# Attention in strict program order with layer 2 in slots beside the heads, and Mamba's side work in other slots

## The chip, the cores and the metric

The kernel runs on one core of a Trainium2 chip. The metric is device time in microseconds of one execution. Times before come from three runs and one profiled execution; a profile is one execution with every instruction recorded. Engines are named as in the profile: PE (matmuls), PEld (PE's weight loads), DVE (vector), ACT (scalar, with the exponentials), POOL (GpSimd), SP (issues DMAs).

## The reference, cut to what matters

For a batch of 8 images of 256 channels and 1024 positions, in float32:

```python
for i in range(4):                                   # four Mamba layers
    xs = xs + mamba(layernorm(xs), ...)              # state scan over 1024 positions, 512 channels x 16 states
y  = xo * sigmoid(se(xo.mean((2, 3)))) + residual    # squeeze and excite
x  = batchnorm(y)                                    # over all 8 images

# layer 1: 4 heads of 64
attn = softmax(einsum('bihd,bjhd->bijh', q, k) * 64 ** -0.5, over j)
x = (attn @ v) @ w_out + b_out + x
# layer 2: one head of 256, and the maximum minus the energy
energy = q @ k.T
attention = softmax(energy.max(-1) - energy)
x = gamma * (attention @ v) + x
# layer 3: 8 heads of 32
tok = x + position_encoding
out = softmax(q @ k.T / 32 ** 0.5) @ v @ Wo + bo
```

## The kernel before

**Two phases.** `mamba_phase` runs the four Mamba layers, the gate and the statistics of the batch norm and leaves y in DRAM (`spill`). `attention_phase` then reads each image back, normalises it and runs the three attention layers. A general attention after it runs only if a range check fails, which it does not with these inputs. At the phases' border the SBUF pools change, so attention's loads start when Mamba's last work is done.

**Order in Mamba.** Its `nc` is `Engines(tc)`: every instruction of PE, DVE, ACT and POOL is kept in program order; SP's DMAs are not. A unit is one half image (512 positions) of one layer: 64 units, each of 16 steps. A step forms two inputs `bx` on PE from a diagonal matrix `dg` and the transposed `dtxT`, scans each on DVE (`h`), multiplies by C on POOL, and sums over states on PE (`y`, three steps later). Beside the steps run the pieces of other units: `inward` (layer norm, input projections `pin`, convolution taps, gate `sz`, projection `pp`) for the unit two ahead, `onward` (`pb`, `pd`, softplus, `dtx`) and `turn` (transposes `pt`) for the next, `outward` (`po`, residual, and in the last layer the gate) for the one before. A unit has 64 slots, four per step, and `BESIDE_SCAN` says at which slot each piece of a stage stands; `DIAGONALS` does so for the loads of `dg`. Slots a and b of a step (0 and 1 modulo 4) stand before its first `bx` and after its second, c and d follow. The small PSUM pool `ps_m` has two buffers, for `pmu`, `pvar`, `pin`, `pp`, `pb`, `pd`, `pt` and `po`.

**Order in attention.** Its `nc` is the plain `tc.nc`: the framework's scheduler puts each engine's instructions in an order of its own choice, within dependencies and the buffers of the pools. The outer order is layer 1 of image 0, layer 1 of image 1, layer 3 of image 0, layer 1 of image 2, layer 3 of image 1, and so on. `heads` (line 643) is the work of one layer 1 or 3: 32 steps, each with scores `fs` for one key tile of 128 and half the queries (line 655; two heads of 64 rows, or four of 32 rows), one or two exponentials to `fp` (660), the product with v to `fo` (671) and the sums of the weights to `fz` (677, on DVE, and for the second pair of heads on POOL). Every eighth step the sums are added over partitions by a matmul with ones (`fzs`, 688), inverted (690) and multiplied in (692), and POOL checks their range (695, 696). `LAG` is the number of steps by which product and sum follow the scores.

Beside the heads of one layer runs `beside(i)` (line 787): the end of the layer before (`residual`, then all of `layer2`; or `output`) and the beginning of the layer after (`begin`: load, batch norm, q, k, v; or q, k, v of layer 3), as one sequence of pieces, dealt out evenly by the counts in `BESIDE`. `layer2` goes over eight query tiles: energies (735) into a score buffer, minimum (738), exponential with sum (741), a diagonal matrix `dg` with gamma over the sum (747), the transpose and scaling in one as a matmul with `dg` (753), two copies (754), the product with v (759), the residual (761).

Score buffers `ps_s`: two, of 128x1024, for `fs` of layers 1 and 3 and for layer 2's energies. All other PSUM tiles of attention: four buffers of `ps_o`. The pool `pp` has six buffers for `fp`, each with the weights of one pair of heads in one step.

Of the kernel before, what the change touches and what calls it, by code (L numbers as in the profile page):

```python
# [12 lines left out]
F32 = mybir.dt.float32  # L13
AF = mybir.ActivationFunctionType
# [5 lines left out]
P = 128  # L20
# [32 lines left out]
class Engines:  # L53
# [12 lines left out]
BESIDE_SCAN = (  # L66
    ("weights", 2, (2, 2, 3, 4)),
    ("onward", 1, (3, 5, 8, 12, 12, 13, 21, 25, 27, 31, 35, 35, 41, 46, 46, 51)),
    ("turn", 1, (49, 51, 55, 57)),
    ("outward", -1, (6, 12, 16, 18, 21, 29, 31, 32, 39, 43, 50, 51, 55, 55, 61)),  # L70
    ("inward", 2, (2, 4, 7, 10, 16, 21, 23, 25, 28, 34, 40, 40, 44, 44, 44, 46, 49, 59, 63)),
)

DIAGONALS = (16, 20, 36, 40, 44, 48, 52, 56)

# [481 lines left out]

LAG = {1: 3, 2: 2}

BESIDE = {(0, 1): 13, (1, 3): 49, (1, 1): 50, (3, 3): 16, (3, 0): 4}  # L560


def attention_phase(tc, ctx, a, spill, ident, gvec, stats, out, top):

    nc = tc.nc
    cst = ctx.enter_context(tc.tile_pool(name="f_cst", bufs=1))
    xp = ctx.enter_context(tc.tile_pool(name="f_x", bufs=4))
    qp = ctx.enter_context(tc.tile_pool(name="f_q", bufs=3))
    kp = ctx.enter_context(tc.tile_pool(name="f_k", bufs=2))
    pp = ctx.enter_context(tc.tile_pool(name="f_p", bufs=6))  # L570
    zp = ctx.enter_context(tc.tile_pool(name="f_z", bufs=3))
# [9 lines left out]

    w = {k: load(k, [P, CT, C], a[k]) for k in ATT_W if k not in ("wq2", "wk2")}
    pe = load("pe", [P, CT, HW], a["pe"])
    bv = {n: load(f"bv{n}", [P, C], a[f"bv{n}"].partition_broadcast(P)) for n in (1, 2, 3)}
    gamma = load("gamma", [P, 1], a["gamma"].partition_broadcast(P))
    ones = cst.tile([P, 64], F32, name="ones")
    nc.gpsimd.memset(ones, 1.0)
    ok = cst.tile([P, T], F32, name="ok")
    nc.gpsimd.memset(ok, 1.0)
    mv, bsc = bn_scale(nc, cst, gvec, stats)  # L590

    def gcol(i):
        return gvec[:, i:i + 1]

    rows = [load(k, [P, CT, C], a[k]) for k in ("wq2_rows", "wk2_rows")]
    w["wq2"] = cst.tile([P, CT, C], F32, name="wqk2")
    bias2 = cst.tile([P, CT], F32, name="bias2")
    for m in range(CT):  # L600
        ps = ps_o.tile([P, T], F32, name=f"wqk2_{m}", tag="o")
        for k in range(CT):
            nc.tensor.matmul(ps[:, :C], lhsT=rows[0][:, k, m * P:(m + 1) * P], rhs=rows[1][:, k, :],
                             start=(k == 0), stop=(k == CT - 1))
        nc.vector.tensor_copy(w["wq2"][:, m, :], ps[:, :C])
        ps = ps_o.tile([P, T], F32, name=f"bias2_{m}", tag="o")
        for k in range(CT):
            nc.tensor.matmul(ps[:, :1], lhsT=rows[1][:, k, m * P:(m + 1) * P], rhs=gcol(G_BQ2 + k),
                             start=(k == 0), stop=(k == CT - 1))
        nc.vector.tensor_copy(bias2[:, m:m + 1], ps[:, :1])  # L610

# [30 lines left out]
    def heads(n, b, s, D, scale):  # L642
# [20 lines left out]
        def product(i):  # L663
            m, half, kt = steps[i]
            if kt == 0:
                acc["o"] = ps_o.tile([P, T], F32, name=f"fo{u}_{m}_{half}", tag="o")
                acc["z"] = [zp.tile([P, 2, T], F32, name=f"fz{u}_{m}_{half}_{j}", tag="z") for j in range(pairs)]
            ps = probs[i]
            for h in range(2 * pairs):
                r = h * D  # L670
                nc.tensor.matmul(acc["o"][r:r + D, :], lhsT=v[:, kt, m * P + r:m * P + r + D], rhs=ps[h // 2][:, h % 2, :],  # L671
                                 start=(kt == 0), stop=(kt == TT - 1))

            if kt:
                for j in range(pairs):
                    add = nc.gpsimd.tensor_tensor if j else nc.vector.tensor_tensor
                    add(acc["z"][j], acc["z"][j] if kt > 1 else probs[i - 1][j], ps[j], ALU.add)  # L677
                del probs[i - 1]

        def divide(i):  # L680
            m, half, kt = steps[i]
            if kt < TT - 1:
                return
            del probs[i]
            z = ps_o.tile([P, T], F32, name=f"fzs{u}_{m}_{half}", tag="o")
            for h in range(2 * pairs):
                r = h * D
                nc.tensor.matmul(z[r:r + D, :], lhsT=ones[:, :D], rhs=acc["z"][h // 2][:, h % 2, :], start=True, stop=True)  # L688
            rec = sp.tile([P, T], F32, name=f"frec{u}_{m}_{half}", tag="rec")
            nc.vector.reciprocal(rec, z)  # L690

            nc.vector.tensor_tensor(q[:, m, half * T:(half + 1) * T], acc["o"], rec, ALU.mult)
            for op, bound in ((ALU.is_le, 1e25), (ALU.is_ge, 1e-37)):
                f = sp.tile([P, T], F32, name=f"fok{u}_{m}_{half}_{bound}", tag="f")
                nc.gpsimd.tensor_scalar(f, rec, bound, None, op)
                nc.gpsimd.tensor_tensor(ok, ok, f, ALU.mult)

        lag = LAG[pairs]
        for i in range(len(steps) + lag + 1):
            if i < len(steps):  # L700
                weights(i)
            if 0 <= i - lag - 1:
                divide(i - lag - 1)
            if lag <= i < len(steps) + lag:
                product(i - lag)
            yield

# [18 lines left out]
    def layer2(b, x):  # L726
        s = {}
        yield from qkv(2, b, x, bias2, None, s)
        q, v = s["q"], s["v"]
        for t in range(TT):  # L730
            u = f"{b}_{t}"
            sc = ps_s.tile([P, 2, T], F32, name=f"fs2{u}", tag="s")
            for half in range(2):
                for m in range(CT):
                    nc.tensor.matmul(sc[:, half, :], lhsT=q[:, m, t * P:(t + 1) * P], rhs=x[:, m, half * T:(half + 1) * T],  # L735
                                     start=(m == 0), stop=(m == CT - 1))
            e = l2.tile([P, 1], F32, name=f"fe2{u}", tag="e")
            nc.vector.tensor_reduce(e, sc, AX.XY, ALU.min)
            p = l2.tile([P, HW], F32, name=f"fp2{u}", tag="p2")
            z = l2.tile([P, 1], F32, name=f"fz2{u}", tag="z")  # L740
            nc.scalar.activation(p, sc.rearrange("p h t -> p (h t)"), AF.Exp, bias=e, scale=-1.0, accum_out=z)  # L741
            yield

            rz = l2.tile([P, 1], F32, name=f"frz2{u}", tag="rz")
            nc.vector.reciprocal(rz, z)
            dg = l2.tile([P, P], F32, name=f"fdg2{u}", tag="dg")
            nc.vector.tensor_scalar(dg, ident, rz, gamma, ALU.mult, ALU.mult)
            pt = l2.tile([P, TT, P], F32, name=f"fpt2{u}", tag="pt")
            for g in range(2):
                ps = ps_o.tile([P, TT // 2, P], F32, name=f"ft2{u}_{g}", tag="o")  # L750
                for j in range(TT // 2):
                    kt = g * TT // 2 + j
                    nc.tensor.matmul(ps[:, j, :], lhsT=p[:, kt * P:(kt + 1) * P], rhs=dg, start=True, stop=True)  # L753
                nc.vector.tensor_copy(pt[:, g * TT // 2:(g + 1) * TT // 2, :], ps)
            yield
            po = ps_o.tile([P, CT, P], F32, name=f"fo2{u}", tag="o")
            for m in range(CT):
                for kt in range(TT):
                    nc.tensor.matmul(po[:, m, :], lhsT=v[:, kt, m * P:(m + 1) * P], rhs=pt[:, kt, :],  # L759
                                     start=(kt == 0), stop=(kt == TT - 1))  # L760
            nc.vector.tensor_tensor(s["q"][:, :, t * P:(t + 1) * P], po, x[:, :, t * P:(t + 1) * P], ALU.add)
            yield
# [3 lines left out]

    xs = {}

    def begin(b, s):
        x = xs[b] = xp.tile([P, CT, HW], F32, name=f"fx{b}", tag="x")  # L770
        for h in range(NCH):
            nc.sync.dma_start(x[:, :, h * T:(h + 1) * T], spill[b][h])
        for m in range(CT):
            nc.vector.tensor_scalar(x[:, m, :], x[:, m, :], mv[:, m, 0:1], bsc[:, m:m + 1], ALU.subtract, ALU.mult)
            nc.vector.tensor_scalar(x[:, m, :], x[:, m, :], gcol(G_BNB + m), None, ALU.add)
        yield
        yield from qkv(1, b, x, gvec[:, G_BQ1:G_BQ1 + CT], gvec[:, G_BK1:G_BK1 + CT], s)
# [8 lines left out]

    def beside(i):
        if i:
# [4 lines left out]
            else:  # L793
                yield from output(b, state[3, b])
        if i + 1 < len(order):
            n, b = order[i + 1]
# [5 lines left out]
    for _ in begin(0, state[1, 0]):  # L802
        pass
    for i, (n, b) in enumerate(order):
        side = beside(i)
        D = 64 if n == 1 else 32
        count = CT * 2 * TT
        work = BESIDE[(order[i - 1][0] if i else 0, order[i + 1][0] if i + 1 < len(order) else 0)]
        done = 0
        for g, _ in enumerate(heads(n, b, state[n, b], D, D ** -0.5)):  # L810
            while done * count < work * (g + 1):
                next(side, None)
                done += 1
        for _ in side:
            pass
# [304 lines left out]
```

## Time and profile before

| what | value |
|---|---|
| runs | 9191.63, 9197.91, 9198.4 us, median 9197.91 |
| profiled execution | 9194.97 us |
| its span, first to last instruction | 9193.1 us |
| last PE work of Mamba ends (`se`) | about 6543 us |
| first attention matmul (`wqk`) starts | 6574.01 us |
| first projection of layer 1 (`fwq`) starts | 6580.22 us |
| layer 3's heads of image 1 (with layer 2 of image 2 beside them) | 7223.4 to 7447.2 us |
| layer 1's heads of image 3 | 7447.2 to 7546.9 us |
| mean granted clock of PE | 0.975 |

The page's lines for groups name the line of the kernel, engine, operation, output and inputs, shapes, and the idle time before. In Mamba all lines are L48, the helper that records each operation, so groups are told apart by their tiles. A float32 matmul shows as two PE instructions.

What some groups of attention cost (from 7000 to 9000 us; busy us, mean ns, then idle before and what ended it):

```profile
L660 ACT ACTIVATE fp<-fs 128x1024 f32<-128x1024 f32 x592 | 590.2, 1022 | 1096.8 <-PE fs L655 1085.5 <-POOL ok L696 11.3
L677 POOL TENSOR_TENSOR fz<-fz,fp 128x1024 f32<-128x1024 f32 x149 | 366.6, 2461 | 373.8 <-ACT fp L660 371.9
L690 DVE RECIPROCAL frec<-fzs 128x512 f32<-128x512 f32 x49 | 164.5, 3356 | 58.0 <-PE fzs L688 57.1
L753 PE MATMUL ft<-fdg,fp 128*128 128x128 f32 x816 | 115.1, 297 | 3.8 <-DVE frec L690 3.8
L747 DVE TENSOR_SCALAR fdg<-ident,frz,gamma 128x128 f32<-128x128 f32 x52 | 18.0, 346 | 1.9
```

### The profile page before, as it was taken

Reading aid. Unit: us, or ns where it says so; the run is one execution under the profiler, and the core shown is the slowest. Engines: PE = TensorE matmul, PEld = TensorE weight load, DVE = VectorE, ACT = ScalarE, POOL = GpSimd, SP = SyncE. Lnnn points to the kernel's source line nnn. Section 1 sums busy time; section 2 is a strip of 40 time slices with the busy share of each in tenths; the row PEclk is TensorE's granted clock in tenths of the full one; section 3 lists DMA queues with packets and bytes.
Section 4 is the critical chain, followed back from the end, with each engine's and each line's share of the span. In section 5 each row is a group of like instructions: output and inputs, shape, how many; then the busy total and the mean of one; then the engine's idle time right before and its main releaser. Section 6 shows DMA issues by size and latency. Waiting matters only on the chain.

```text
span 9193.1 us, 231133 instructions
## 1 busy us (share of the span) xinstructions
PE 8829.2 (96%) x100850; PEld 4513.2 (49%) x100850; DVE 7154.2 (78%) x7267; ACT 5369.8 (58%) x7646; POOL 7009.5 (76%) x2696
## 2 busy tenths in 40 slices
PE   8999999999999999999999999999799999999998
PEld 4555555555555555555555555555344334434433
DVE  5898988889888898989889999999654554455455
ACT  6667676766776676676667677767323333333334
POOL 5999999999999999999999999999414343343436
PEclk8999999999999999999999999999999999999999
DMA  3434434443443444344444444444200000000000
GB/s 108 129 120 122 124 122 127 121 127 122 122 122 124 127 121 127 122 122 123 123 127 121 137 134 134 135 130 141 99 1 5 10 10 5 5 5 5 1 5 10
DMA packets 559192, 845.58 MB, mean 92 GB/s; under 512 B 311456, under 2 KB 312544, under 8 KB 557536
## 3 DMA queue, kind: packets, MB, share of 16 engines
q1 hardware_dynamic: 558176, 830.71, 29.6%
q8 instruction: 799, 13.09, 0.6%
q14 instruction: 217, 1.78, 0.1%
HBM read 771.31 MB, written 59.24 MB: 90 GB/s over the span
## 4 chain that ended last, share of the span: by engine, by line
PE 86%; DVE 6%; ACT 3%; POOL 2%; issue 2%; DMA 0%; SPq 0%; ACTq 0%; DVEq 0%; POOLq 0%
PE bx L48 20%; PE y L48 19%; PE pin L48 10%; PE fs L655 6%; PE po L48 5%; PE fo L671 4%; DVE h L48 3%; PE fo L759 3%; PE pp L48 3%; PE fs L735 3%; PE pd L48 2%; PE fwq L615 2%; PE fwv L637 2%; PE ft L753 1%; PE pvar L48 1%
## 5 line engine op out<-in xcount | busy, mean ns | idle before, releaser
L48 POOL TENSOR_TENSOR h<-h,ct 128x2048 f32<-128x2048 f32 x1024 | 4640.3, 4544 | 451.9 <-PE y L48 161.3
L48 ACT ACTIVATE da<-dt,A 128x512 f32<-128x512 f32 x4096 | 2642.6, 713 | 224.9 <-DVE h L48 222.6
L48 DVE TENSOR_TENSOR_SCAN h<-da,hc,bx 128x512 f32<-128x512 f32 x2048 | 2456.8, 1261 | 238.8 <-PE bx L48 228.4
L48 DVE TENSOR_TENSOR_SCAN h<-da,bx 128x512 f32<-128x512 f32 x2048 | 2356.9, 1203 | 281.1 <-PE bx L48 266.3
L48 PEld LDWEIGHTS bx<-dg,dtxT 64*64 64x64 f32 x65536 | 1915.0, 135 | 1264.1 <-issue 1178.1
L48 PE MATMUL bx<-dg,dtxT 64*64 64x128 f32 x65536 | 2253.4, 276 | 39.7 <-DVE h L48 28.8
L48 PE MATMUL y<-h,twin 64*64 64x512 f32 x16384 | 2018.8, 608 | 6.1 <-POOL h L48 6.1
L660 ACT ACTIVATE fp<-fs 128x1024 f32<-128x1024 f32 x768 | 765.6, 1022 | 1426.3 <-PE fs L655 1398.0
L48 PE MATMUL pin<-xn,win 128*128 128x512 f32 x2048 | 1009.2, 616 | 61.4 <-ACT sz L48 49.4
L48 PEld LDWEIGHTS y<-h,twin 64*64 64x64 f32 x16384 | 616.1, 138 | 675.6 <-issue 665.8
L677 POOL TENSOR_TENSOR fz<-fz,fp 128x1024 f32<-128x1024 f32 x192 | 478.1, 2490 | 414.5 <-ACT fp L660 410.5
L677 DVE TENSOR_TENSOR fz<-fz,fp 128x1024 f32<-128x1024 f32 x384 | 531.8, 1385 | 328.0 <-ACT fp L660 323.7
L655 PE MATMUL fs<-fq,fk 32*128 32x512 f32 (+1 forms) x3072 | 718.0, 646 | 54.9 <-ACT fp L741 39.3
L48 DVE SCALAR_TENSOR_TENSOR xin<-pin,vec,xin 128x509 f32<-128x509 f32 (+2 forms) x768 | 571.6, 744 | 100.3 <-ACT xin L48 42.8
L671 PE MATMUL fo<-fp,fv 128*32 128x512 f32 (+1 forms) x3072 | 596.6, 615 | 0.0
L48 PEld LDWEIGHTS pin<-xn,win 128*128 128x128 f32 x2048 | 355.6, 191 | 457.9 <-issue 330.4
L48 ACT ACTIVATE xin<-pin,cb,vec 128x512 f32<-128x512 f32 x256 | 199.2, 778 | 621.8 <-PE pin L48 621.8
L48 PE MATMUL po<-sz,wo 128*128 128x512 f32 x1024 | 500.7, 612 | 0.0
L48 ACT ACTIVATE sz<-pin,ib 128x512 f32<-128x512 f32 x256 | 175.9, 687 | 549.8 <-PE pin L48 549.8
L655 PEld LDWEIGHTS fs<-fq,fk 32*128 32x128 f32 (+1 forms) x3072 | 195.3, 185 | 467.8 <-issue 271.0
L677 POOL TENSOR_TENSOR fz<-fp,fp 128x1024 f32<-128x1024 f32 x32 | 83.1, 2597 | 403.2 <-PE fzs L688 240.8
L48 ACT ACTIVATE e<-pd,vec 128x512 f32<-128x512 f32 x256 | 176.1, 688 | 317.4 <-PE pd L48 312.5
(391 smaller groups left out, 8743.4 us busy)
## 6 DMA issues: line engine op xcount, KB each, us to landing
ct<-cdr SPq DMA_DIRECT2D x1024, 512.0 KB, 3.9
dg<-diagonals SPq DMA_DIRECT2D x512, 256.0 KB, 4.3
spill<-xo SPq DMA_DIRECT2D x72, 512.0 KB, 5.3
x<-spill SPq DMA_DIRECT2D x48, 512.0 KB, 7.8
xo<-spill SPq DMA_DIRECT2D x48, 512.0 KB, 5.0
x<-in_x SPq DMA_DIRECT2D x16, 512.0 KB, 8.4
res<-in_x SPq DMA_DIRECT2D x16, 512.0 KB, 5.1
diagonals<-bt SPq DMA_DIRECT2D x512, 4.0 KB, 4.6
```

The costliest lines, as they stand in the source:

```text
L48: return self.tc.keep_in_program_order(getattr(self.engine, name)(*args, **kwargs))
L615: nc.tensor.matmul(ps, lhsT=wt[:, k, m * P:(m + 1) * P], rhs=x[:, k, half * T:(half + 1) * T], start=(k == 0), stop=(k == CT - 1))
L637: nc.tensor.matmul(ps[:, j, :], lhsT=x[:, kc, (t + j) * P:(t + j + 1) * P], rhs=w[f"wv{n}"][:, kc, :], start=(kc == 0), stop=(kc == CT - 1))
L655: nc.tensor.matmul(scs[h // 2][:, h % 2, :], lhsT=k[r:r + D, m, kt * P:(kt + 1) * P], rhs=q[r:r + D, m, half * T:(half + 1) * T], start=Tr ...
L660: nc.scalar.activation(p, scs[j], AF.Exp, scale=scale)
L671: nc.tensor.matmul(acc["o"][r:r + D, :], lhsT=v[:, kt, m * P + r:m * P + r + D], rhs=ps[h // 2][:, h % 2, :], start=(kt == 0), stop=(kt == ...
L677: add(acc["z"][j], acc["z"][j] if kt > 1 else probs[i - 1][j], ps[j], ALU.add)
L735: nc.tensor.matmul(sc[:, half, :], lhsT=q[:, m, t * P:(t + 1) * P], rhs=x[:, m, half * T:(half + 1) * T], start=(m == 0), stop=(m == CT - 1))
L753: nc.tensor.matmul(ps[:, j, :], lhsT=p[:, kt * P:(kt + 1) * P], rhs=dg, start=True, stop=True)
L759: nc.tensor.matmul(po[:, m, :], lhsT=v[:, kt, m * P:(m + 1) * P], rhs=pt[:, kt, :], start=(kt == 0), stop=(kt == TT - 1))
```

## The change

In attention `nc` becomes `Engines(tc)`: strict program order on PE, DVE, ACT and POOL. The order within a step is written out in `PARTS_H` (fs: scores and exponentials, fo: product and sums, z: division; 0, 1, 2: slots for pieces), `LAG` is 1, and where the neighbours are the regular ones `BESIDE_H` names the slot (three per step, 96 in all) of each piece of the layer before ("end", with layer 2 in it) and of the layer after ("begin"). Elsewhere 52 pieces are dealt out evenly. Layer 2 is cut into more pieces, staggered over query tiles; gamma over the sum is applied on ACT to the weights before they are turned, and the turning is `tensor.transpose` with the identity. The batch norm moves from DVE to ACT. The weights' pool has eight buffers. Image 0 and the weights of its q, k and v are loaded first; the other weights, and the fused q-k weight of layer 2, come after the first projections. In Mamba the slots of the pieces change.

```diff
 BESIDE_SCAN = (
-    ("weights", 2, (2, 2, 3, 4)),
-    ("onward", 1, (3, 5, 8, 12, 12, 13, 21, 25, 27, 31, 35, 35, 41, 46, 46, 51)),
-    ("turn", 1, (49, 51, 55, 57)),
-    ("outward", -1, (6, 12, 16, 18, 21, 29, 31, 32, 39, 43, 50, 51, 55, 55, 61)),
-    ("inward", 2, (2, 4, 7, 10, 16, 21, 23, 25, 28, 34, 40, 40, 44, 44, 44, 46, 49, 59, 63)),
+    ("weights", 2, (0, 2, 2, 7)),
+    ("onward", 1, (1, 3, 6, 8, 8, 16, 21, 25, 27, 31, 35, 35, 41, 45, 46, 51)),
+    ("turn", 1, (46, 49, 56, 58)),
+    ("outward", -1, (6, 13, 16, 20, 23, 30, 32, 33, 37, 41, 48, 50, 53, 53, 61)),
+    ("inward", 2, (0, 0, 3, 10, 15, 19, 19, 29, 29, 34, 40, 43, 44, 44, 44, 46, 49, 59, 63)),
 )
-DIAGONALS = (16, 20, 36, 40, 44, 48, 52, 56)
+DIAGONALS = (12, 20, 36, 40, 44, 48, 52, 56)
...
-LAG = {1: 3, 2: 2}
-BESIDE = {(0, 1): 13, (1, 3): 49, (1, 1): 50, (3, 3): 16, (3, 0): 4}
+LAG = {1: 1, 2: 1}
+PARTS_H = {1: ("fs", "z", "fo", "0", "1", "2"), 2: ("0", "fs", "fo", "z", "1", "2")}
+BESIDE_H = {
+    3: (("end", (3, 5, 6, 8, 10, 14, 15, 15, 16, 22, 27, 28, 28, 28, 28, 29, 30, 42, 42, 42, 44, 48, 48, 50, 52, 54, 59, 59, 60, 62, 65, 66, 68, 69, 69, 75, 76, 76, 80, 83)),
+        ("begin", (40, 44, 50, 52, 55, 55, 63, 70, 78, 83, 86, 88, 91))),
+    1: (("end", (16, 16, 38, 41)),
+        ("begin", (37, 39, 43, 44, 52, 56, 64, 74, 79, 83, 87, 89))),
+}
+PIECES = 52
...
-    nc = tc.nc
+    nc = Engines(tc)
...
-    pp = ctx.enter_context(tc.tile_pool(name="f_p", bufs=6))
+    pp = ctx.enter_context(tc.tile_pool(name="f_p", bufs=8))
...
         lag = LAG[pairs]
         for i in range(len(steps) + lag + 1):
-            if i < len(steps):
-                weights(i)
-            if 0 <= i - lag - 1:
-                divide(i - lag - 1)
-            if lag <= i < len(steps) + lag:
-                product(i - lag)
-            yield
+            for part in PARTS_H[pairs]:
...
+                else:
+                    yield 3 * i + int(part)
...
-            dg = l2.tile([P, P], F32, name=f"fdg2{u}", tag="dg")
-            nc.vector.tensor_scalar(dg, ident, rz, gamma, ALU.mult, ALU.mult)
...
-                    nc.tensor.matmul(ps[:, j, :], lhsT=p[:, kt * P:(kt + 1) * P], rhs=dg, start=True, stop=True)
...
+        def scale(t):
+            z = es.pop((t, "z"))
+            nc.vector.reciprocal(z, z)
+            rz = l2.tile([P, 1], F32, name=f"frz2{b}_{t}", tag="rz")
+            nc.scalar.activation(rz, z, AF.Identity, scale=gamma)
+            nc.scalar.activation(ps[t], ps[t], AF.Identity, scale=rz)
...
+                    nc.tensor.transpose(tr[:, j, :], p[:, kt * P:(kt + 1) * P], ident)
...
+        for i in range(TT + 2):
+            if i < TT:
+                energies(i)
+                yield
+            if 0 <= i - 2:
+                product(i - 2)
+            if i < TT:
+                weights(i)
+            yield
+            if 0 <= i - 1 < TT:
+                turn(i - 1)
+            if i < TT:
+                scale(i)
             yield
...
-            nc.vector.tensor_scalar(x[:, m, :], x[:, m, :], mv[:, m, 0:1], bsc[:, m:m + 1], ALU.subtract, ALU.mult)
-            nc.vector.tensor_scalar(x[:, m, :], x[:, m, :], gcol(G_BNB + m), None, ALU.add)
+            nc.scalar.activation(x[:, m, :], x[:, m, :], AF.Identity, bias=nmu[:, m:m + 1])
+            nc.scalar.activation(x[:, m, :], x[:, m, :], AF.Identity, scale=bsc[:, m:m + 1], bias=gcol(G_BNB + m))
...
+        regular = 0 < i and i + 1 < len(order) and order[i - 1][0] == order[i + 1][0] == (3 if n == 1 else 1)
+        for slot in heads(n, b, state[n, b], D, D ** -0.5):
+            if regular:
+                for (what, when), g in zip(BESIDE_H[n], (ends, nexts)):
+                    for _ in range(when.count(slot)):
+                        next(g, None)
+            else:
+                while count * 96 < PIECES * slot:
+                    next(both, None)
+                    count += 1
```

## The prediction, made before the run

> **What bounds the kernel now.** First the page: busy shares and the 40 slices.
>
> ```profile
> PE 8829.2 (96%) x100850; PEld 4513.2 (49%) x100850; DVE 7154.2 (78%) x7267; ACT 5369.8 (58%) x7646; POOL 7009.5 (76%) x2696
> ...
> PE   8999999999999999999999999999799999999998
> ...
> DVE  5898988889888898989889999999654554455455
> ACT  6667676766776676676667677767323333333334
> POOL 5999999999999999999999999999414343343436
> ```
>
> PE is at nine tenths throughout. In the Mamba phase (28 slices, to about 6543 us) DVE and POOL are close behind it; in attention (the rest) nothing else passes two thirds in a slice. The table by stretches says the same with numbers: a piece of Mamba, one stretch of layer 3's heads (layer 2 of the next image lies beside it), one of layer 1's heads.
>
> ```profile
> 2000.00:4000.00 2000.00, 1949.94 (x27660) 1063.42 (x27652) 1793.71 (x1828) 1399.23 (x2079) 1845.03 (x676) 0.98 0.41 124
> 7223.40:7447.20 223.80, 213.28 (x1122) 101.22 (x1120) 103.45 (x112) 71.89 (x80) 99.39 (x45) 0.99 0.00 1
> 7447.20:7546.90 99.70, 99.70 (x360) 31.39 (x356) 62.87 (x52) 32.63 (x32) 29.99 (x16) 1.00 0.06 22
> ```
>
> (Columns: stretch, length, busy of PE, weight loads, DVE, ACT, POOL, clock, DMA share, GB/s.) So time is PE time, and a busy PE has to be looked into. The timeline of PE over one query tile of layer 2 beside layer 3's heads:
>
> ```profile
> 6971.45 3.70 PE L735 MATMUL fs<-fx,fq 128*128 128x512 f32 x8
> 6975.08 1.13 PE L655 MATMUL fs<-fq,fk 32*128 32x512 f32 x4
> 6976.14 1.04 PE L671 MATMUL fo<-fp,fv 128*32 128x512 f32 x2
> 6977.70 1.13 PE L655 MATMUL fs<-fq,fk 32*128 32x512 f32 x4 [0.52 <-ACT fp L741]
> 6978.76 1.06 PE L671 MATMUL fo<-fp,fv 128*32 128x512 f32 x6
> 6979.75 2.05 PE L753 MATMUL ft<-fdg,fp 128*128 128x128 f32 x16
> 6981.69 3.84 PE L759 MATMUL fo<-fpt,fv 128*128 128x128 f32 x32
> 6985.46 1.14 PE L655 MATMUL fs<-fq,fk 32*128 32x512 f32 x8
> 6986.53 1.07 PE L671 MATMUL fo<-fp,fv 128*32 128x512 f32 x8
> ```
>
> Eight instructions of four heads (two per float32 matmul) take 1.07 us from start to next start, and so do four of two heads: a step whose heads are split pays twice. And in Mamba, waits of PE (us, times, longest; 200 to 6400 us) and the place of the first:
>
> ```profile
> PE pd L48 <- ACT dt L48: 86.7, 61, 1.7
> PE pin L48 <- ACT sz L48: 47.5, 61, 0.8
> PE bx L48 <- DVE h L48: 16.2, 56, 0.6
> ```
>
> ```profile
> 3171.95 1.12 PE L48 MATMUL pd<-proj,wdt 16*128 16x512 f32 x2
> 3174.49 1.12 PE L48 MATMUL pd<-proj,wdt 16*128 16x512 f32 x2 [1.42 <-ACT dt L48]
> 3175.54 1.10 PE L48 MATMUL bx<-dg,dtxT 64*64 64x128 f32 x32
> ```
>
> [...] four heads cost what two do, and a run followed by another mode costs 0.15 to 0.20 us more than its instructions (fo of two heads 1.01 us, against 3.48 us for sixteen in a row, 0.87 per four). [...] The trace has both: Mamba's pt takes one instruction per 128x128 block, ft takes two. [...]
>
> **The change, part by part.** The built programs can be laid side by side, so I count runs of equal tiling mode on PE, from the first attention matmul to the last.
>
> *Heads kept together.* Before, the scheduler splits steps of the heads around waits. A float32 128x512 matmul streams 2 x 0.4285 = 0.857 us (weight loads of po stand 0.43 apart), and heads in different tiles share that. By this rate the old order streams layer 3's fs, fo, fzs in 290.5 + 255.4 + 34.3 us over eight images, layer 1's fs in 226.2; the new order, in which every step has its heads in one run, in 219.4 + 219.4 + 27.4 and 219.4. Saved: 121 us.
>
> *Fewer changes of mode.* 1529 runs become 1308; at 0.15 to 0.21 each by mode, 279 us become 236. Saved: 43 us.
>
> *Transposes.* 64 query tiles x 8 blocks. ft: 16 instructions in 1.94 to 1.98 us, some 1.8 without the change of mode. pt: four blocks in 0.49 to 0.58 us, eight in 1.05 with the change of mode; so 0.9. Saved: 64 x 0.9 = 58 us. Bounds: 50 (pt's 0.49 doubled, nothing overlapping) to 62.
>
> *Work moved to ACT.* Normalising x: 4 ACTIVATEs of 128x1024 per image, about 1.02 us each by fp's row (1022 ns); 1/z and gamma: one of 1.02 and one of about 0.2 us per query tile. Together 8 x 4.1 + 64 x 1.22 = 111 us. DVE loses the fdg (346 ns x 64) and the two tensor_scalars (809 + 698 ns, x16). ACT is busy for 72 of 224 us in the stretch concerned: hidden. Without that cover it costs where a head's exp queues behind it: 1 to 2 us of PE per query tile, up to 100 us. Nothing is gained by DVE's relief, PE being the bound.
>
> *Waits of attention.* The counts give 2453 us for the old order; the trace has 2611 from 6574 to 9185. The 158 between are listed idle (88 us, half of it fs waiting for layer 2's exp), a last stretch (8837 to 9185) limited by POOL and by p buffers (3.95 us waits), and clock. In the new order the energies of a query tile and the scores that reuse their buffer have, but for the first pair of tiles, a 3.7 us product run between them, so the 0.5 us waits of line 655 on line 741 should go. New ones come: a layer 3 step with no piece in it is bound by two exps before its score buffers return (in the last stretch of before such steps took 2.3 to 2.9 us against 2.07 of PE), and some five steps per image are bare; a lone transpose run (1 us) leaves about 0.5. LAG 1 adds none: between a step's scores and its product stand one product and one score run, 2.07 us, against 1.02 of exp. Eight p buffers, four steps, let POOL run behind (25.2 us of POOL per eight steps against 30.1 now): some 17 us off the last stretch. I take the sum of waits as 148, ten less; bounds 90 and 230.
>
> *The start.* x and three weights are loaded first, 1.75 MB in place of about 4.9 (192 GB/s in that stretch: 9 us and not 25), fwq can start some 7 us sooner; the fused weights' matmuls (4.4 us), till now in the shade of the loads, come after. Saved: 3 us. SP only issues in another order, and later loads have 20 us of projections to land in.
>
> Attention: -121 - 43 - 58 - 10 - 3 = -235 us.
>
> *Mamba's slots.* The pd of the second half stood between pin1 and the taps that release its PSUM buffer, so its two matmuls shared one buffer: 1.06, idle 1.42, 1.06. In the new slots (pd at 27, pin1 and its taps both at 29) no half-used buffer is held there: 1.06 in all, as 3138.91 shows for four instructions. Saved per unit: 2.5 us. The pair of the first half now follows pb directly; its second matmul needs pb's copy by ACT (0.19 us, but in 3233.97 it came 1.1 us after pb): costs 0.3 to 1.2, I take 0.4. PE sees 133 fewer changes of mode, of which I count one pair per unit, 0.27. Net 2.3 x 62 units = 145 us of PE. DVE (1794 of 2000) and POOL (1845) then stand at 92 to 95% of the shortened time and will not follow everywhere; moved pieces also put taps right behind their projection, where DVE waits for PE and ACT. I take two thirds: -100 us. Bounds: -160, and +50 should DVE's new waits win. Loads moved to slot 0 cost nothing: the order of SP's instructions issues x a unit (100 us) ahead of its use.
>
> Sum: -335 us on the profiled execution's 9194.97 (its span 9193.1 and 1.9 around it): 8860. The median of the runs is 2.9 higher, 9197.91: 8863, rounded to 8865.
>
> **Rivals.**
> A, the forecast, both phases gain: 8865 (8800 to 8930), chance 0.57.
> B, attention gains, Mamba nothing: POOL at 92% and DVE at 90% become the bound as soon as PE is relieved. For it: their shares; against it: PE waits for DVE only 16 us and DVE for PE hundreds. 9198 - 235 = 8963. Chance 0.2.
> C, strict order gives back over half of attention: ACT and DVE blocked by layer 2's reciprocal, scale or maximum, then scores, 2 us at each of 64 tiles, 128 us, and Mamba half: 9198 - 107 - 50 = 9040. For it: [...] a reciprocal of 3.36 us on DVE; against: all three engines idle over half. Chance 0.13.
> D, both more: waits of attention at 90, Mamba in full, transposes at 62: 8740 to 8790. Chance 0.05.
> E, slower: DVE in Mamba. Taps at the slot of their projection (19, 29) hold DVE for PE's 1.9 and ACT's 0.8 us, and pp with pmu now keeps bx away from it for 5.5 us. A unit takes 99.7 us (the first pd run starts at 3138.91 and, a unit on, at 3238.56), DVE is busy for 89.5 of them (1793.7 of 2000); to outweigh attention's 235 us each of 62 units must grow by 3.8, so DVE's idle must go from 10 to 14 us. From there on slower; I put it at 9250. Chance 0.05. That the slots don't move anything is excluded by the two orders.
>
> **Numbers.** No change cannot be told from 0.2% either way (18 us). Faster 0.94, same 0.02 (between C and E), slower 0.04. The range 8780 to 9000 takes in A, B and the near end of D, and leaves out C and E, less than 2 in 10.
>
> **What would show it.** Right: fs of layer 3 always in runs of eight; ft with 512 instructions, eight in about 1 us; a layer 3 stretch of about 195 us (223.8 now) and layer 1 still near 100; no wait of pd on ACT's dt, a Mamba unit near 98.1 us (99.7 now); DVE's and ACT's waits there not grown. Wrong: layer 3 stretches above 210, with fs waiting for fp; Mamba units at 99.7 or more with PE idle for h from DVE or POOL.

## The result, and the profile after

The changed kernel takes 8765.76 us (median of 4 runs, 8759.97 to 8766.57), the kernel before 9197.44 beside it: ratio 0.9531, 95% interval 0.9514 to 0.9547. That is 432 us off, 99 more than forecast, and 14 us below the low end of the range. The last Mamba instruction of PE (`se`) ends at 6543.0 us before and at 6331.9 after; by this split Mamba lost 211 us (forecast 100) and attention 217 (forecast 235).

The page of the kernel after, busy shares and slices:

```profile
PE 8440.6 (96%) x100338; PEld 4363.7 (50%) x100338; DVE 7196.5 (82%) x7171; ACT 5500.7 (63%) x7807; POOL 6960.2 (79%) x2696
...
PE   7999999999999999999999999999799999999998
...
DVE  5999999999999999999999999999755655565555
ACT  6777777777777777777777777777533344434434
POOL 5999999999999999999999999999813444343436
```

Its table by stretches (columns as before): two thousand microseconds of Mamba, a stretch of layer 3's heads, one of layer 1's, and the last of all from the start of layer 3's heads of image 6.

```profile
2000.00:4000.00 2000.00, 1952.62 (x28625) 1082.35 (x28629) 1863.92 (x1893) 1450.36 (x2152) 1908.41 (x699) 1.00 0.42 128
6957.44:7145.67 188.23, 185.12 (x1059) 88.59 (x1057) 106.29 (x100) 87.51 (x100) 92.09 (x44) 1.00 0.00 1
7145.67:7245.68 100.01, 99.45 (x354) 31.39 (x352) 65.54 (x52) 32.64 (x32) 31.19 (x17) 1.00 0.06 21
8404.65:8764.80 360.15, 315.99 (x1636) 123.41 (x1634) 186.91 (x148) 145.28 (x160) 209.02 (x93) 0.92 0.02 7
```

In Mamba, PE is busy for as long as before (1950 of 2000 us) and yet computes 3.5% more instructions: the column ahead of the DMA share, the granted clock, went from 0.98 to 1.00. That column was in front of me in the prediction and I passed over it. Layer 3's stretch shrank from 223.8 to 188.2 us. The last row shrank not at all; the same part of the kernel before:

```profile
8837.11:9193.10 355.99, 322.23 (x1700) 128.71 (x1698) 171.88 (x156) 134.96 (x144) 206.89 (x93) 0.96 0.02 7
```

PE is busy for 6 us less there, but the granted clock of the stretch fell from 0.96 to 0.92.

PE's waits in Mamba after, 200 to 6300 us (total, times, longest):

```profile
PE bx L48 <- DVE h L48: 88.1, 128, 4.9
PE pin L48 <- ACT sz L48: 47.4, 61, 0.8
```

The wait of pd (86.7 us) is gone; that of bx for DVE rose from 16.0 to 88.1. Now what the wait of pd cost beyond its own length. The timeline of PE in the kernel before, continued from the lines that the prediction shows, and one like it a unit later:

```profile
3176.47 3.57 PE L48 MATMUL y<-h,twin 64*64 64x512 f32 x16
...
3275.19 1.72 PE L48 MATMUL bx<-dg,dtxT 64*64 64x128 f32 x32
3276.67 3.03 PE L48 MATMUL y<-h,twin 64*64 64x512 f32 x16
```

And the same place in the kernel after:

```profile
3064.60 1.13 PE L48 MATMUL pd<-proj,wdt 16*128 16x512 f32 x4
3065.65 1.10 PE L48 MATMUL bx<-dg,dtxT 64*64 64x128 f32 x32
3066.58 1.90 PE L48 MATMUL y<-h,twin 64*64 64x512 f32 x16
```

The same sixteen instructions take 3.57 us and not 1.90. The trace's records of the granted clock say why: PE runs at half its clock for 3.41 us after the wait (stretches of the kernel before, columns as above):

```profile
3173.13:3176.54 3.41, 2.05 (x38) 1.29 (x42) 3.31 (x5) 2.15 (x4) 3.41 (x3) 1.00 0.16 58
3176.54:3179.95 3.41, 3.41 (x24) 1.05 (x20) 2.43 (x3) 3.41 (x6) 3.41 (x2) 0.50 0.74 253
```

A busy PE is all that the shares show of it. I summed this over both traces, from 1000 to 6300 us: whatever a run of PE took above the median of runs of its kind and length, where that is over 0.4 us. Before: 114.7 us in 119 runs, 112.8 of them right after a pd; after: 9.0 us in 8 runs. Below I call this the half-clock excess. The clock records agree: between 1000 and 6300 us the kernel before spends 242 us at half clock, so loses 121, and the kernel after spends 24.

### The profile page after: what moved, and what is told of

It reads as the page before. It is cut to its first block, busy times and chain, and to the rows that moved or that the text cites. A ratio compares the mean times of both kernels' runs of the same rounds, so it can differ in the third digit from the quotient of the medians.

```text
span 8764.8 us, 230661 instructions
## 1 busy us (share of the span) xinstructions
PE 8440.6 (96%) x100338; PEld 4363.7 (50%) x100338; DVE 7196.5 (82%) x7171; ACT 5500.7 (63%) x7807; POOL 6960.2 (79%) x2696
## 4 chain that ended last, share of the span: by engine, by line
PE 81%; DVE 10%; ACT 3%; issue 3%; POOL 2%; DMA 0%; SPq 0%; POOLq 0%; DVEq 0%; ACTq 0%
PE bx L48 18%; PE y L48 17%; PE pin L48 9%; PE fs L48 9%; DVE h L48 8%; PE fo L48 8%; PE po L48 5%; PE pp L48 3%; PE fwv L48 2%; PE fwq L48 2%; PE pd L48 2%; PE pvar L48 1%; PE fwk L48 1%; PE pmu L48 1%; PE fpo L48 1%
## 5 line engine op out<-in xcount | busy, mean ns | idle before, releaser
L48 PEld LDWEIGHTS bx<-dg,dtxT 64*64 64x64 f32 x65536 | 1885.4, 133 | 1303.5 <-issue 1049.0
L48 DVE TENSOR_TENSOR_SCAN h<-da,bx 128x512 f32<-128x512 f32 x2048 | 2358.5, 1204 | 127.2 <-PE bx L48 114.7
L48 PE MATMUL bx<-dg,dtxT 64*64 64x128 f32 x65536 | 2222.9, 273 | 120.2 <-DVE h L48 93.3
L48 PE MATMUL y<-h,twin 64*64 64x512 f32 x16384 | 1959.0, 591 | 4.8 <-POOL h L48 4.8
L48 PE MATMUL fs<-fq,fk 32*128 32x512 f32 (+1 forms) x3072 | 638.2, 657 | 29.9 <-ACT fp L48 28.2
L48 DVE TENSOR_TENSOR fz<-fz,fp 128x1024 f32<-128x1024 f32 x384 | 597.9, 1557 | 78.8 <-ACT fp L48 69.8
L48 PE MATMUL fo<-fp,fv 128*32 128x512 f32 (+1 forms) x3072 | 566.2, 624 | 3.1 <-ACT fp L48 1.6
L48 POOL TENSOR_TENSOR e<-e,one 128x1024 f32<-128x1024 f32 x128 | 303.8, 2373 | 76.4 <-ACT one L48 63.8
L48 ACT COPY dtxT<-pt 128x512 f32<-128x512 f32 x256 | 149.9, 586 | 333.3 <-PE pt L48 333.3
```

What stands on the lines that cost most here:

```text
L48: return self.tc.keep_in_program_order(getattr(self.engine, name)(*args, **kwargs))
```

## The experiments

Theory W: the second pd's wait, with all that follows from it (idle, two serial products, half clock), carries most of Mamba's 211 us. Theory R: the wait is worth its listed idle and the serial pair, and the rest comes from merged pieces and other slots. The rest of the questions: what starts the half clock, and which of attention's terms hold.

**e1 and e2: each phase alone.** e1 is the kernel before with the new `BESIDE_SCAN` and `DIAGONALS`; e2 the changed kernel with the old ones.

> The kernel before with only the two tables of Mamba's slots replaced by the new ones. Both theories: about 9197 - 211 = 8986 us, if the split of the two traces at the last Mamba instruction of PE holds (before about 6543, after about 6332) and the phases don't act on each other. If the granted clock in Mamba depends on what runs later or on the order of attention, less: 9090 or so.

> The changed kernel with Mamba's two slot tables as before. Both theories: 9197 - 217 = 8980 us; Mamba ends near 6543 again, pd waits for ACT some 61 times, the clock in Mamba is 0.98.

e1: 8988.92 us, ratio 0.9778 (0.9762 to 0.9795), half-clock excess 8.8 us. e2: 8972.26 us, 0.9760 (0.9744 to 0.9777), half-clock excess 117.0 us. The two halves, 206 and 223 us, add up to the whole within 3 us: the phases can be studied apart, and the half clock in Mamba goes with Mamba's slots, whichever attention follows.

**e3: the taps ahead of pd.**

```diff
-    ("inward", 2, (2, 4, 7, 10, 16, 21, 23, 25, 28, 34, 40, ...
+    ("inward", 2, (2, 4, 7, 10, 16, 21, 23, 25, 26, 34, 40, ...
```

> The kernel before with one number changed: the second taps of a unit's input at slot 26 and no longer 28, so that they stand ahead of the second pd (27) and both PSUM buffers are free for it. Theory W (the wait of pd is the cause of nearly all that Mamba gained: 1.42 us idle + 1.06 us of serial pair + 1.65 us of half clock after it, 4.1 us in each of 62 units, of which DVE and POOL give back a part): 170 to 230 us off, 8970 to 9030; the clock in Mamba rises from 0.98 to 1.00 and y runs of over 2.5 us become rare. Theory R (the wait is worth its listed idle and the serial pair alone, with a third lost as I had taken it: some 100 us; the rest of Mamba's 211 comes from merged pieces and other slots, the slow y runs among them): 9090 to 9130, clock still 0.98 to 0.99.

9194.85 us, ratio 1.000 (0.9991 to 1.0009), pd's wait and the half-clock excess (116.1) as before. Neither theory had this, and the run tests neither: its trace has the same instructions in the same order as the kernel before on every engine. The queue of DVE in e3 shows why:

```profile
3168.74 4.54 DVE L48 TENSOR_TENSOR_SCAN h<-da,bx 128x512 f32<-128x512 f32 x4
3173.31 0.16 DVE L48 TENSOR_REDUCE hc<-h 128x4 f32<-128x4 f32 x1
3173.39 2.31 DVE L48 SCALAR_TENSOR_TENSOR xin<-pin,vec,xin 128x509 f32<-128x509 f32 x3
```

The taps stand behind four scans on DVE whether their slot is 26 or 28. PE is two to three microseconds ahead of DVE there, so the buffer of pin1 is still taken when pd comes (3171.01). It is pin1 that has to move, not its taps.

**e5: pin1 and its taps behind pd.** In the kernel before:

```diff
-    ("inward", 2, (2, 4, 7, 10, 16, 21, 23, 25, 28, 34, 40, ...
+    ("inward", 2, (2, 4, 7, 10, 16, 21, 23, 29, 29, 34, 40, ...
```

> The kernel before with two numbers changed: the second input projection and its taps at slot 29 (they were at 25 and 28), behind the second pd (27), so that no half-used PSUM buffer is held while pd runs. In e3 the taps moved ahead in the text and on no engine: on DVE they stand behind the scans of the same step either way, so the buffer stayed taken; this is the edit that frees it. Theory W (wait of pd with all that follows from it: 1.42 us idle, 1.06 us of serial pair, some 2 us of half clock, 4.5 us per unit, part of it lost to DVE and POOL): 150 to 240 us off, 8955 to 9045, clock in Mamba 1.00, slow runs (115 us of excess between 1000 and 6300 us in the kernel before) below 20 us. Theory R (listed idle and serial pair alone): 60 to 110 us off, slow runs stay.

9005.04 us, ratio 0.9792 (0.9776 to 0.9808): 193 us from two numbers, 94% of what all of Mamba's new slots bring (e1). The half-clock excess is 7.9 us, the clock 1.00, and pd's wait is gone; two others grew, yet neither brings a half-clock run (waits of PE, 200 to 6300 us):

```profile
PE bx L48 <- PE pd L48: 55.8, 61, 0.9
PE pin L48 <- ACT sz L48: 47.4, 61, 0.8
PE bx L48 <- DVE h L48: 43.8, 116, 1.1
```

R is out.

**e4: the conflict put back into the changed kernel.**

```diff
-    ("inward", 2, (0, 0, 3, 10, 15, 19, 19, 29, 29, 34, ...
+    ("inward", 2, (0, 0, 3, 10, 15, 19, 19, 25, 29, 34, ...
```

> The changed kernel with one number changed: the second input projection at slot 25 and no longer 29, its taps still at 29, so that it holds a PSUM buffer while the second pd (27) runs. Theory W: 170 to 230 us more than the changed kernel's 8766, 8935 to 9000; pd waits for ACT some 61 times with 1.4 us, the clock in Mamba falls to 0.98, slow y runs come back. Theory R: 60 to 110 us more, 8825 to 8875, clock 0.99 to 1.00.

9110.39 us, ratio to before 0.9909 (0.9893 to 0.9926): 345 us slower than the changed kernel, half as much again as W said. Its waits:

```profile
PE bx L48 <- DVE h L48: 156.7, 168, 1.6
PE pd L48 <- ACT dt L48: 83.9, 59, 1.7
```

Pd's wait 84, the serial pair 59 x 1.06 = 63, half-clock excess 88.0 less 9.0 in 5300 us, so 91 in 6100, and 69 more of bx waiting for DVE: 307 of 345. The rest I could not place. So the price of such a conflict depends on what surrounds it: 193 us in the old slots, 345 in the new (where the taps stand at 29 and not at 28).

**e6: idle filled with work.** In the kernel before, the second pd's matmuls become pieces of their own:

```diff
-    ("onward", 1, (3, 5, 8, 12, 12, 13, 21, 25, 27, 31, ...
+    ("onward", 1, (3, 5, 8, 12, 12, 13, 21, 25, 27, 29, 31, ...
...
+                nc.scalar.activation(dt[:, r, :], pd, AF.Relu, bias=col(V_DB + i))
+                if q and not r:
+                    yield
```

> The kernel before with the second pd's two matmuls in pieces of their own, at slots 27 and 29: PE computes bx, y, bx between them in place of standing idle; each is alone, so the serial cost of 1.06 us and a change of mode stay. Theory W1 (the idle stretch starts the half clock): idle and slow runs both go, 1.42 + 2.0 - 0.3 = 3.1 us per unit, 120 to 190 us off, 9005 to 9075, clock 1.00. Theory W2 (the thin matmuls, 16 of 128 rows, start it, not the idle): slow runs stay at some 115 us, at most 1.42 x 62 = 88 us off, 9107 to 9150, clock 0.98.

9115.66 us, ratio 0.9909 (0.9892 to 0.9925), half-clock excess 67.3 us: between the two. The idle did not vanish, it changed place, from pd to the bx behind it, and its half clock with it (timeline of PE):

```profile
2243.45 1.12 PE L48 MATMUL pd<-proj,wdt 16*128 16x512 f32 x2
2245.89 1.13 PE L48 MATMUL bx<-dg,dtxT 64*64 64x128 f32 x32 [1.32 <-DVE h L48]
2246.79 3.62 PE L48 MATMUL y<-h,twin 64*64 64x512 f32 x16
```

36 of some 54 units show half-clock runs, against 50 in the kernel before. That lies between W1 and W2 and excludes neither, so the idle was measured by itself.

**e7: idle alone.** This kernel leaves the computation out: on PE only products run, dense work of 40 us between the cases. Its core (`full` is two products of 128 rows, `thin` one of 16 rows, `pause` lets PE idle while ACT works):

```python
one = full if form == "full" else thin
one(mm[1], src)
one(mm[0], pause(mm[1], n, name) if n else src)
```

> Not the computation: only TensorE, dense runs of Mamba's bx and y forms and full 128x512 products (some 40 us), then a product, an idle of PE for one ACTIVATE of a chosen width (none, then 0.4 to 4 us), a second product, and dense runs again; once with full 128-row products around the idle and once with thin 16-row ones as pd's; six times each, shifted by some 0.1 us. Theory W1: y runs after idles of about 1.4 us and more take over 2.5 us (1.9 without) in both forms, and shorter ones leave no mark. Theory W2: only in the thin form, and there without an idle too. A third case: whether a slow run follows is a matter of where the idle falls, so that at 1.0 to 3 us some of the six are slow and others not, the share growing with length.

How often, of six, a half-clock run followed (counted from the trace, 5225 us):

| idle, us | none | 0.37 | 0.98 | 1.13 | 1.35 | 1.56 | 1.77 | 2.20 | 2.73 | 3.59 |
|---|---|---|---|---|---|---|---|---|---|---|
| full products around it | 0 | 0 | 0 | 0 | 0 | 0 | 0 | 0 | 4 | 5 |
| thin products around it | 0 | 4 | 4 | 4 | 5 | 6 | 5 | 6 | 6 | 5 |

A case of each kind (timeline of PE: full with 2.20 us, which leaves no mark; full with 2.73; thin with 1.35):

```profile
359.31 1.98 PE L22 MATMUL mm<-src,full 128*128 128x512 f32 x4 [2.20 <-ACT full L22]
361.22 1.10 PE L22 MATMUL bx<-src 64*64 64x128 f32 x32
362.15 1.90 PE L22 MATMUL y<-src 64*64 64x512 f32 x16
...
402.38 3.52 PE L22 MATMUL mm<-src,full 128*128 128x512 f32 x4 [2.73 <-ACT full L22]
...
651.24 2.07 PE L22 MATMUL mm<-src,thin 16*128 16x512 f32 x2 [1.35 <-ACT thin L22]
653.23 1.99 PE L22 MATMUL bx<-src 64*64 64x128 f32 x32
655.00 3.43 PE L22 MATMUL y<-src 64*64 64x512 f32 x16
```

Neither W1 nor W2 as I put them: 1.42 us of idle is not enough alone (none of 42 cases up to 2.20 us), and thin products are not either (none of six without idle). Together they are. A thin product takes 1.1 us, so thin, 0.37, thin is 2.6 us of little work, and half clock follows about as often as after 2.73 us of nothing.

The clock records settle why some cases of a kind have it and others not. In all 13 traces here the granted clock is 1.00 or 0.50, and it changes only at the steps of a grid of 3.413 us that runs through the whole execution (every change lies within 0.02 us of a step). For each stretch between two steps that ran at full clock I added up the time in which PE was idle or ran thin products (in Mamba pd and pb on 16 rows, and `pib` of 128x1), and looked at the clock of the next stretch:

| idle and thin time in a stretch, us | under 1.9 | 1.9 to 2.1 | over 2.1 |
|---|---|---|---|
| e7, 60 to 5200 us: next at full clock, at half | 1353, 0 | 9, 2 | 0, 53 |
| before, e4, e5, e6, e8 and after, 1000 to 6300 us | 8924, 0 | 36, 8 | 0, 153 |

So in these traces half clock followed when some 2 us of one stretch of 3.4 were idle or thin, the two counted alike, and it lasted to the next step at least (in the kernel before 3.41 us in 46 of 82 cases, 6.83 in 32). A wait that falls across a step is shared between two stretches, and in this way it left no mark three times in the kernel before (pd at 4784.76: 1.93 us idle or thin in one stretch, 1.59 in the next, no half clock). It fits the units of the kernels: before, 1.06 + 1.42 + 1.06 = 3.5 us, half clock in 50 of some 54 units; e6, 1.06 + 1.32 = 2.4, in 36; e5, 1.06 + 0.9 = 2.0, in none. How the weight of a product falls with its rows was not varied between 16 and 128.

**e8: one more conflict of that kind.** The z projections' wait for ACT (47 us) is the same figure: two products that share a buffer.

```diff
-    ... 34, 40, 43, 44, 44, 44, 46, 49, 59, 63)),
+    ... 34, 40, 43, 44, 44, 45, 46, 49, 59, 63)),
```

> The changed kernel with one number changed: the second of the four z projections at slot 45 and no longer 44, with bx, y, bx ahead of it, so that PE needn't wait for ACT to read the first one (0.78 us in each unit, 47 us in all). If PE still sets Mamba's time: 30 to 48 us off, 8718 to 8736. If DVE (93%) and POOL (95%) set it by now: within 12 us of 8766, and PE's waits for DVE grow by what went.

8736.88 us (8736.22 to 8744.18), ratio 0.9501 (0.9485 to 0.9517): 29 us below the changed kernel, for 27 us less of this wait (20.8 are left) and bx's wait for DVE all but unmoved at 90.5. So with DVE at 93% and POOL at 95% busy (2000 to 4000 us of the changed kernel), PE still sets the pace of Mamba: rival B's ground is not there.

**e9: the transposes as products again.**

```diff
-                    nc.tensor.transpose(tr[:, j, :], p[:, kt * P:(kt + 1) * P], ident)
+                    nc.tensor.matmul(tr[:, j, :], lhsT=p[:, kt * P:(kt + 1) * P], rhs=ident, start=True, stop=True)
```

> The changed kernel with layer 2's 512 transposes issued as products with the identity again (two instructions of a float32 product and not one). My term for them was 58 us (50 to 62) of PE: 8816 to 8830. If the slots leave PE slack at those places (a lone transpose run had room beside it), under 25 us: 8766 to 8790.

8824.70 us, ratio 0.9597 (0.9582 to 0.9611): 59 us more, and the groups of PE by form say the same, after and e9:

```profile
L48 PE MATMUL ft<-ident,fp 128*128 128x128 f32 x512 | 71.9, 282 | 0.1
```

```profile
L48 PE MATMUL ft<-ident,fp 128*128 128x128 f32 x1024 | 131.3, 282 | 0.0
```

**e10: attention back to the scheduler.**

```diff
-    nc = Engines(tc)
+    nc = tc.nc
```

> The changed kernel with attention's instructions handed to the scheduler again and not held in program order; pieces, slots, buffers and transposes stay. By my count of tiling modes and streams on the built program PE then has 2272 us in place of 2229: splits of layer 3's steps return in part. If keeping order is worth its count: +43, about 8809 (8795 to 8825). If order also saves waits: over 8830. If the new pieces and slots alone carry the gain, or strict order costs waits: 8766 or less.

8759.49 us, ratio 0.9526 (0.9511 to 0.9540): the same time as the changed kernel. As counted, PE has more to do: after Mamba it has 1365 runs of equal mode and not 1309, and is busy for 2345.0 us, against 2325 to 2334 in the changed kernel and in e2, e4 and e8, whose attention is the same. But its listed idle is 67 us and not 87 to 90 (waits of fs for ACT 14.3 and not 31.7 in the changed kernel), and 72 us in place of 96 to 112 ran at half clock. The length of attention is 2424.0 us, and 2424.1 to 2432.9 in those four: no difference. Strict order by itself is worth nothing here: what it saves in splits it gives back in waits. The rest of the change carries attention's gain; of it only the transposes were measured alone.

**e11: the last stretch.** With e8's edit, and:

```diff
-                    add = nc.gpsimd.tensor_tensor if j else nc.vector.tensor_tensor
+                    add = nc.gpsimd.tensor_tensor if j and not (n == 3 and b == B - 1) else nc.vector.tensor_tensor
```

> e8 (8737 us) with one more edit: in the last stretch of heads (layer 3, image 7) all sums of probabilities on VectorE, none on GpSimdE. There GpSimdE takes 18.86 us for six adds of 128x1024 while VectorE adds too, 2.4 alone, and sets the pace at some 31 us per group of eight steps; VectorE alone takes 14 x 1.22 + 3.4 + 0.7 = 21 us a group and PE about 20. Theory P (GpSimdE is why the last stretch did not shrink): three to four groups by some 10 us, 30 to 40 off, 8697 to 8707. Rival (VectorE is no faster alone than beside GpSimdE, 1.6 us and more an add): 27 us a group, 8 to 15 us off, 8722 to 8729.

8714.12 us (8710.03 to 8723.74), ratio 0.9480 (0.9467 to 0.9493), the fastest of all. First POOL, DVE and PE of the changed kernel in that stretch:

```profile
8631.37 18.86 POOL L48 TENSOR_TENSOR fz<-fz,fp 128x1024 f32<-128x1024 f32 x6 [3.03 <-ACT fp L48]
```

```profile
8635.33 12.68 DVE L48 TENSOR_TENSOR fz<-fz,fp 128x1024 f32<-128x1024 f32 x4 [0.53 <-ACT fp L48]
```

```profile
8665.96 2.99 PE L48 MATMUL fs<-fq,fk 32*128 32x512 f32 x8 [4.19 <-ACT fp L48]
8668.89 1.94 PE L48 MATMUL fo<-fp,fv 128*32 128x512 f32 x8
...
8746.33 1.92 PE L48 MATMUL fzs<-fz,ones 128*32 128x512 f32 x4 [5.99 <-POOL fz L48]
```

An add is 3.14 us on POOL and 3.17 on DVE when both add at once; fs waits 4.19 us (its exp, on ACT, waits for POOL to free a buffer of p) and then runs at half clock (0.50 from 8665.96 to 8668.90). In e11 DVE does it alone:

```profile
8627.44 15.22 DVE L48 TENSOR_TENSOR fz<-fz,fp 128x1024 f32<-128x1024 f32 x12
```

That is 1.27 us an add. GpSimdE alone takes 2.35 (at 8569.53 in the changed kernel), so one add of each in turns would make 3.6 us; side by side the pair takes some 3.15, and DVE alone would do two in 2.54. What slows the engines beside each other is not shown. In e11 a group of eight steps takes 23.8 us (8619.89 to 8643.70, starts of its first fs) in place of 32.3 (8651.27 to 8683.55). The total gained 23 us over e8 by the medians, 27 by the profiled spans and 19 by the ratios to the kernel before: theory P by mechanism, under its 30 to 40, since a group costs 24 and not 21. Part of the gain is half clock that goes with the waits: PE spends 51 us of the last stretch at half clock in e8 and 21 in e11.

## Why the prediction was right or wrong

- *Heads kept together, fewer changes of mode (-164), transposes (-58).* Right in kind: fs of layer 3 stands in 256 runs of eight, runs of equal mode went from 1530 to 1309, and the transposes are shown to be 59 (e9). The sum was too high: PE's busy time after Mamba fell by 188 us (2521.5 to 2333.6) and not by 222. Strict order is only part of what keeps the heads together: without it 230 of the 256 runs of eight remain (e10), and the loss of the others cost no time.
- *Waits of attention -10.* Too low: PE's listed idle after Mamba, without the wait for the first load, fell from 88.6 to 63.4 us. The reason given for 17 of it was wrong, though: what bounds the last stretch is not the number of p's buffers but POOL and DVE adding at once (e11), and it went from 356 to 360 us although PE has less to stream. That attention as a whole came so near the forecast (-217 for -235) is in part luck: these two errors offset each other.
- *The start -3.* Nearer 8: the first fs comes 50.9 us after Mamba's end, 59.4 before.
- *Mamba: pd's wait.* The place and the mechanism were right, wait and serial pair go as I said (2.5 us a unit), and e5 shows that they are the heart of it. **The step that failed is the size of this term**: I priced a wait at its listed length, and put the half clock behind it at nothing. It is 114.7 us of half-clock excess in 5300 before and 9.0 after; the difference is 122 us over the phase, 2 us in each unit, about the 111 us by which the term fell short.
- *"I take two thirds".* Right in kind, too little in size. The sum would have been 145 + 122 = 267, and 211 came, 79%. The first pair of pd behind pb costs what I took: pb and pd last 1.77 us together, against 0.35 + 1.06 before, so 0.36 more. What did take some back is DVE: PE's bx waits 88 us for it and not 16. Yet DVE did not become the bound, as e8 shows.
- *"DVE's and ACT's waits there not grown".* Right as written: between 200 and 6300 us DVE's waits fell from 554 to 349 us (behind PE's bx from 457 to 180), and ACT's fell too. What grew is PE's waits for DVE, which I had named as a sign of being wrong, beside units of 99.7 us or more: they came and were outweighed, a unit takes 96.8 us (median) where 98.1 was forecast.
- *Rivals.* The range of D (8740 to 8790, chance 0.05) holds the result, but not for D's reasons: attention gave no more than forecast, and all the excess came from Mamba, most of it from the half clock, which D did not have. B, nothing from Mamba, did not come. C's point, strict order that gives back over half of attention, did not show; E's DVE bound neither.

That a wait of 1.42 us costs its own length and no more was an estimate of mine, which no trace had shown. The clock column, 0.98 in Mamba and 0.99 to 1.00 in layers 3 and 1, said that something follows it.

## What to carry to other kernels

Price a wait on the busiest engine with what runs after it, not with its own length: compare the duration of the next runs with the same runs elsewhere, and ask for the reason wherever the granted clock is below 1.00 in a stretch without long gaps (0.98 here). Add up idle and thin products that stand close together; here some 2 us of them within one 3.4 us stretch cost another 1.7. Where two products share a PSUM buffer, look for the product ahead of them whose reader is late on its own queue; moving that product and its reader behind them is two numbers in a table and was worth nearly as much here as all moves of the phase together (193 of 206 us). Put no wait beside products that use few rows (16 here: with 0.37 us between two of them half clock followed in 4 of 6 cases), and don't share a stream of adds between VectorE and GpSimdE where together they are no faster than VectorE alone (here 0.63 adds per us together, 0.79 alone).

## What the runs showed that I had not expected

- Idle and thin products add up: 16-row products with 0.37 us between them cost half clock in 4 of 6 cases, full ones with 2.20 us in none of 6. Over 2.1 us of both in one stretch of the 3.413 us grid was followed by half clock in all 206 cases of seven traces, under 1.9 us in none of 10277.
- A float32 add of 128x1024 takes 1.27 us on VectorE alone, and 3.17 on VectorE with 3.14 on GpSimdE when both add; together they do 0.63 adds per us, VectorE alone 0.79.
- Much the same conflict differs in price by almost two: taking it out of the old slots gains 193 us (e5), putting it into the new costs 345 (e4).
